# Row ends of a four-layer modulated convolution, as corrections subtracted at the end

## The chip, the cores and the metric

One core of one Trainium2 chip. The metric is the time of the program on the device in microseconds, the median of its runs. The engines are TensorE (PE, with its weight loads as PEld), VectorE (DVE), ScalarE (ACT), GpSimd (POOL), and SyncE (SP), which here issues nearly all DMAs.

## The reference

x is 128 x 64 x 1024 (batch, channels, length), fp32; cond_512 (128 x 128) is the style.

```python
def _layer(x, style, w, b, mw, mb, typ):
    s = style @ mw.T + mb
    weight = SCALE * w * s[:, None, :, None]
    demod = lax.rsqrt(jnp.sum(weight * weight, axis=(2, 3)) + EPS)
    weight = weight * demod[:, :, None, None]
    if typ == 'same':
        out = conv_same(x, weight) + b
    elif typ == 'upsample':
        out = conv_transpose(x, weight, stride 2) + b
        out = _blur(out, 2.0 * blur_k, (1, 1))
    elif typ == 'downsample':
        xb = _blur(x, blur_k, (2, 2))
        out = conv(xb, weight, stride 2) + b
    return out
...
for i, typ in enumerate(('same', 'upsample', 'same', 'downsample')):
    out = _layer(out, style, weights[i], biases[i], mod_w[i], mod_b[i], typ)
return x + out
```

Each batch element has its own 64 x 64 x 3 weights in every layer. Away from the row ends the four layers are one linear map: a convolution of seven taps of 64 x 64 matrices for each batch element, plus a constant. Within three columns of either end the zero padding of each layer makes the result differ from that convolution.

## The kernel before

**Tiling.** The batch is worked in 32 quads of four (NQ = 32, index q). A quad's two pairs lie side by side in a tile; in a pair, one batch element has partitions 0 to 63 (T) and the other 64 to 127 (Bo). All matmuls are fp32, 64 x 64, in the four quadrants of the array: row half r by column half c. HB is 64, half of the batch.

**The convolution.** x comes in three planes, columns of the same remainder modulo 3 (PL = 344 columns each, two pairs in X, double buffered). A short-convolution scheme makes five products a quad (conv0 to conv4, each 3 groups of four matmuls of NB = 340 columns) from sums of planes: in_g01 and in_g2 write G; in04, in1, in2 and in3 write the T tiles. VectorE does these, but in1 and in2, which run on GpSimd in the middle turns. The products are put together by copy_m3, sum1, sum2 and `output` (ScalarE, PSUM to the tile o, scaled and with the constant), and `store` sends o away. Ahead of this a chain of small matmuls (stage1, stage2, stage3, with combine_a and combine_b) makes the quad's seven-tap weights.

**Order.** The schedule is written out by hand. `turn_of(q)` holds, for q from 4 to 28, a whole turn: conv2, conv4 and conv0 of quad q, conv3 and conv1 of n = q+1, the weights of c = q+2 and s = q+4. `early_turn` does quads 0 to 3, and straight code the last three. Each engine runs its own instructions in program order. PSUM: two buffers for the products (psA; `banks(q)` is quad q's two banks), two banks Y, the rest for the weight chain. Tables SIDE, TABLES and SLOTS hang small work onto certain turns.

**The row ends.** They are computed apart. Eight columns of each end of x (Xe, with zero columns around them) are scaled by the style (setup_x) and go through the four layers for all 128 batch elements at once: ends0 in the slot of turn 10 gives six columns of layer 1, ends1 in turns 14 and 15 nine columns of layer 2 (five and four), ends2 in turn 19 eight columns of layer 3, three steps of the blur on VectorE (blur_side) in turns 22 to 27, and ends3 in the turn of q = 28. Each slot's matmuls go into Y (ends3: into psE), and rest0 to rest3 copy them to SBUF with a scale; add0, rest1_bias, rest1_edges and add2 add the biases. rest3_bias adds the bias and x in the last quads, and two stores send the three outer columns of each end. The convolution covers 1020 columns, of which 1018 are used. In the code of a slot turn:

```python
outputs(q, 0)
if q in SLOTS:
    matmuls, width, rest = SLOTS[q]
    slot(matmuls, width, Y_banks)
    rest()
...
conv1(n, ...)
sum1(n)
in3(c)
```

Lines that the profile names: L803 the convolution's products, L880 output on ScalarE, L712 sums with a factor (G, H, y, Y), L761 in3, L776 in1, L781 in2, L790 in04, L506 and L589 stage2, L428 stage1, L621 stage3, L1044 the end matmuls, L1146 and L1158 the last steps of the ends, L146 loads, L885 stores.

Of the kernel before, what the change touches and what calls it, by code (L numbers as in the profile page):

```python
# [63 lines left out]
def kernel(  # L64
# [74 lines left out]
    Xs = [const.tile([P, 2, NXC], F32, name=f"X{i}") for i in range(NX)]  # L139
# [24 lines left out]
    Xe = const.tile([P, B, 8], F32, name="Xe")  # L164
# [9 lines left out]
    NB = 340  # L174
# [578 lines left out]
    def g_tile(q):  # L753
        if q not in Gs:
            Gs[q] = gpool.tile([P, 2, 3 * PL], F32, tag="G", name=f"G{q}")
        return Xs[q % NX], Gs[q]
# [26 lines left out]
    def in04(q, pairs=BOTH_PAIRS):  # L783
        if q < NQ:
            t, g = t_tile(q, "T04"), Gs[q]
            a, b = g[:, pairs, :NJ], g[:, pairs, 2 * PL : 2 * PL + NJ]
# [3 lines left out]
            nc_v.tensor_sub(t[:, pairs, :, :NJ], both(a, PL), both(b, 1))  # L790
# [102 lines left out]
    WIDE = 6  # L893
    ends_ps = {}

    def slot(matmuls, n, ps, wide=WIDE):
        matmuls(ps)
        ends_ps[0] = ps, max(n, wide)

    def last(i, n, j):  # L900
        ps, w = ends_ps[0]
        return ps[i][:, : n * w].rearrange("c (b j) -> c b j", b=n)[:, :, :j]


# [81 lines left out]
    Xm = const.tile([P, B, 8], F32, name="Xm")  # L986
    Xs0 = [Xm[:, :HB], Xm[:, HB:]]
    a0, c0, a2, c2 = (const.tile([P, HB], F32, name=n) for n in ("a0", "c0", "a2", "c2"))
    g1 = const.tile([P, 6, C], F32, name="g1")

    Ye = [const.tile([P, HB, 8], F32, name=f"Ye{s}") for s in range(2)]
    Ue = [const.tile([P, HB, 11], F32, name=f"Ue{s}") for s in range(2)]
    Ve = [const.tile([P, HB, 12], F32, name=f"Ve{s}") for s in range(2)]
    Oe = const.tile([P, B, 3], F32, name="Oe")

    def zeros():
        for t in Ye:
            nc_g.memset(t[:, :, 0:1], 0.0)
            nc_g.memset(t[:, :, 7:8], 0.0)
        for t in Ue:  # L1000
            nc_g.memset(t[:, :, 0:1], 0.0)
            nc_g.memset(t[:, :, 10:11], 0.0)
        for t in Ve:
            nc_g.memset(t[:, :, 0:2], 0.0)
            nc_g.memset(t[:, :, 10:12], 0.0)
        nc_g.memset(g1, 0.0)

    def spread(t, n):

        return t[:, :, None].to_broadcast([P, t.shape[1], n])  # L1010
# [7 lines left out]
    def setup_x(h):  # L1018
        bs = slice(h * HB, (h + 1) * HB)
        nc_v.tensor_tensor(Xm[:, bs], Xe[:, bs], spread(sc[:, 0, bs], 8), op=ALU.mult)  # L1020

    def setup0():

        for rows, bs in ((T, slice(0, HB)), (Bo, slice(HB, B))):
            nc_v.tensor_mul(a0[rows], dm[rows, 1, bs], dm[rows, 0, bs])
            nc_v.tensor_copy(c0[rows], c0f[rows, bs])
# [4 lines left out]
    def setup3():  # L1031
        for rows, bs in ((T, slice(0, HB)), (Bo, slice(HB, B))):
            nc_v.tensor_copy(a2[rows], Da[rows, bs])
            nc_v.tensor_copy(c2[rows], c2f[rows, bs])

    def ends_matmul(ps, n, taps, weight, moving, wide=WIDE):
        for i in reversed(range(taps)):
            first = i == taps - 1
            w = max(n, wide)
            m = w if first else n  # L1040
            for r, rows in enumerate(HALF):
                for c, cols in enumerate(HALF):
                    dst = ps[r][cols, : HB * w].rearrange("c (b j) -> c b j", j=w)
                    nc.tensor.matmul(  # L1044
                        dst[:, :, :m],
                        weight(i, r, c)[rows],
                        moving(i, r, c, m)[rows],
                        start=first,
                        stop=(i == 0),
                        skip_group_check=True,  # L1050
                    )

    def ends0(ps):

        ends_matmul(
            ps, 6, K, lambda i, r, c: wio[0][:, i, :], lambda i, r, c, m: Xs0[c][:, :, i : i + m]
        )

    def rest0():
        for s in range(2):  # L1060
            dst = Ye[s][:, :, 1:7]
            nc_v.tensor_tensor(dst, last(s, HB, 6), spread(a0, 6), op=ALU.mult)

    def add0(s):
        dst = Ye[s][:, :, 1:7]
        nc_v.tensor_tensor(dst, dst, spread(c0, 6), op=ALU.add)

    def ends1(part):

        n = 5 - part  # L1070


        def weight(i, r, c):
            return g1[:, 2 * i + (part if c == 0 else 1 - part), :]

        def moving(i, r, c, m):
            col = 2 - i + (c + part if c else 0)
            return Ye[c][:, :, col : col + m]

        return lambda ps: ends_matmul(ps, n, K, weight, moving)  # L1080

    def rest1(part):
        n = 5 - part
        for h in range(2):
            bs = slice(h * HB, (h + 1) * HB)
            dst = Ue[h][:, :, 1 + part : 10 : 2]
            nc_v.tensor_tensor(dst, last(h, HB, n), spread(a1[:, bs], n), op=ALU.mult)

    def rest1_bias(h):

        bs = slice(h * HB, (h + 1) * HB)
        dst = Ue[h][:, :, 1:10]
        nc_v.scalar_tensor_tensor(
            dst, spread(b1s[:, bs], 9), 2.0, dst, op0=ALU.mult, op1=ALU.add
        )

    def rest1_edges(h):

        bs = slice(h * HB, (h + 1) * HB)
        for rows, col in ((T, 1), (Bo, 9)):  # L1100
            dst = Ue[h][rows, :, col]
            nc_v.scalar_tensor_tensor(
                dst, b1s[rows, bs], -0.25, dst, op0=ALU.mult, op1=ALU.add
            )

    def ends2(ps):

        ends_matmul(
            ps,
            8,  # L1110
            K,
            lambda i, r, c: wio[2][:, i, :],
            lambda i, r, c, m: Ue[c][:, :, i + r : i + r + m],
        )

    def rest2():
        for s in range(2):
            dst = Ve[s][:, :, 2:10]
            nc_v.tensor_tensor(dst, last(s, HB, 8), spread(a2, 8), op=ALU.mult)

    def add2(s):
        dst = Ve[s][:, :, 2:10]
        nc_v.tensor_tensor(dst, dst, spread(c2, 8), op=ALU.add)


    def blur_side(s, part):
        at = (2 * s, 0, 0)[part]
        src = (Ve[s], Ue[s], Ve[s])[part][:, :, at : at + 10 - part]
        dst = (Ue[s], Ve[s], Ue[s])[part][:, :, : 9 - part]
        nc_v.tensor_tensor(dst, src[:, :, :-1], src[:, :, 1:], op=ALU.add)  # L1130

    def ends3(ps):

        ends_matmul(
            ps,
            3,
            K,
            lambda i, r, c: wio[3][:, i, :],
            lambda i, r, c, m: Ue[c][:, :, i : i + 5 : 2],
            wide=3,  # L1140
        )

    def rest3():
        for h in range(2):
# [577 lines left out]
```

## Time and profile before

| | |
|---|---|
| median of 3 runs | 476.5 us (475.95 to 476.6) |
| span of the profiled execution | 475.5 us |
| PE busy | 469.7 us, 99% |
| VectorE busy | 417.3 us, 88% |
| ScalarE busy | 312.0 us, 66% |
| GpSimd busy | 165.8 us, 35% |
| granted TensorE clock, 40 slices | 0.9 or more in all |
| HBM | 145 GB/s over the span |

The page gives the span of the profiled execution, from its first to its last instruction; the time of that execution as a run isn't shown apart, so its span is set against the median of the runs, 1.0 us over it. Busy time counts an engine as busy while an instruction of it runs, and matmuls overlap. The chain that ended last is followed back from the last instruction; shares of the span by line come from it.

### The profile page before, as it was taken

How to read it: one execution, taken by the hardware profiler on the slowest of the kernel's cores; microseconds unless marked ns; L12 is line 12 of the kernel's file. 1: busy time of each engine (PE TensorE's matmuls, PEld its weight loads, DVE VectorE, ACT ScalarE, POOL GpSimd, SP SyncE). 2: the span in 40 equal slices, each digit the busy share in tenths (PEclk: the TensorE clock that was granted, in tenths of full speed). 3: DMA queues.
4: the chain of work that ended last, by engine and by line, in shares of the span. 5: the costliest groups of instructions: out<-in, count | busy, mean ns of one | idle time of the engine just before them, and what ended most of it. 6: DMA issues, size and time to landing. Idle time of an engine off the chain costs nothing.

```text
span 475.5 us, 26771 instructions
## 1 busy us (share of the span) xinstructions
PE 469.7 (99%) x11932; PEld 349.5 (74%) x11932; DVE 417.3 (88%) x694; ACT 312.0 (66%) x711; POOL 165.8 (35%) x200
## 2 busy tenths in 40 slices
PE   9999999999999999999999999999999999999996
PEld 6987788777678876677776677766788787876653
DVE  3889998879989998899979899979998999999896
ACT  4565657577766676766667666667666777766464
POOL 3634033664444342233432233422333423243200
PEclk9999999999999999999999999999999999999999
DMA  5237456535445554345544454543555544455225
GB/s 176 71 115 224 150 151 180 152 113 177 139 145 166 166 166 136 123 150 169 163 150 126 130 168 152 178 124 121 152 164 169 164 145 147 148 152 161 80 91 193
DMA packets 52707, 70.71 MB, mean 149 GB/s; under 512 B 6000, under 2 KB 50672, under 8 KB 52592
## 3 DMA queue, kind: packets, MB, share of 16 engines
q1 hardware_dynamic: 52368, 68.78, 46.3%
q8 instruction: 93, 1.52, 1.4%
q10 hardware_dynamic: 224, 0.22, 0.1%
q14 instruction: 22, 0.18, 0.1%
HBM read 35.36 MB, written 33.62 MB: 145 GB/s over the span
## 4 chain that ended last, share of the span: by engine, by line
PE 99%; DVE 0%; ACT 0%; issue 0%
PE psA L803 47%; PE Y L803 12%; PE psR L506 9%; PE psW L621 7%; PE psA L621 7%; PE psS L428 6%; PE psR L589 5%; PE psA L506 2%; PE Y L1044 2%; PE Y L183 1%; PE Y L379 1%; PE psM L220 0%; PE psE L1044 0%; PE Y L255 0%; DVE o L882 0%; PE psM L255 0%
## 5 line engine op out<-in xcount | busy, mean ns | idle before, releaser
L803 PE MATMUL psA<-T,H 64*64 64x340 f32 x2304 | 185.9, 446 | 0.0
L803 PEld LDWEIGHTS psA<-T,H 64*64 64x64 f32 x2304 | 90.7, 133 | 46.9 <-issue 2.5
L712 DVE SCALAR_TENSOR_TENSOR G<-X 128x1376 f32<-128x1376 f32 (+2 forms) x65 | 78.0, 1206 | 0.2
L776 POOL TENSOR_TENSOR T<-G 128x684 f32<-128x684 f32 x28 | 46.3, 1652 | 73.7 <-DVE G L712 73.7
L484 POOL TENSOR_TENSOR S<-S 128x128 f32<-128x128 f32 x28 | 21.6, 772 | 139.7 <-ACT S L399 139.6
L399 ACT ACTIVATE R<-psR,tC 128x448 f32<-128x448 f32 x63 | 36.6, 631 | 43.6 <-PE psR L506 25.8
L803 PE MATMUL psA<-T,Wf 64*64 64x340 f32 x768 | 63.7, 446 | 0.0
L803 PE MATMUL Y<-T,Wf 64*64 64x340 f32 x768 | 62.4, 451 | 0.0
L712 DVE SCALAR_TENSOR_TENSOR Y<-m,psA 128x340 f32<-128x340 f32 x62 | 32.0, 516 | 28.2 <-PE psA L803 26.9
L399 ACT ACTIVATE psW<-psA 128x128 f32<-128x128 f32 x100 | 19.3, 268 | 49.1 <-PE psA L621 45.0
L790 DVE TENSOR_TENSOR T<-G 128x1368 f32<-128x1368 f32 (+1 forms) x33 | 50.8, 1541 | 0.0
L399 ACT ACTIVATE Wf<-psW,t 128x256 f32<-128x256 f32 (+2 forms) x76 | 32.7, 480 | 26.7 <-PE psW L621 26.4
L761 DVE TENSOR_TENSOR T<-X 128x684 f32<-128x684 f32 x32 | 47.7, 1492 | 0.0
L506 PE MATMUL psR<-S,E 64*64 64x64 f32 (+1 forms) x1472 | 46.8, 237 | 0.0
L781 POOL TENSOR_TENSOR T<-G 128x684 f32<-128x684 f32 x28 | 46.5, 1660 | 0.0
L428 PEld LDWEIGHTS psS<-wd,w2n 64*64 64x64 f32 x1120 | 35.1, 133 | 12.9 <-issue 0.3
L506 PEld LDWEIGHTS psR<-S,E 64*64 64x64 f32 x1472 | 39.5, 134 | 4.9 <-ACT psR L529 0.2
L803 PEld LDWEIGHTS Y<-T,Wf 64*64 64x64 f32 x768 | 30.3, 132 | 16.8
L803 PEld LDWEIGHTS psA<-T,Wf 64*64 64x64 f32 x768 | 29.8, 133 | 14.5
L880 ACT ACTIVATE o<-psA,tb,td 128x340 f32<-128x340 f32 x63 | 37.1, 648 | 5.0 <-PE psA L803 2.8
L880 ACT ACTIVATE o<-y,tb,td 128x340 f32<-128x340 f32 x62 | 38.5, 678 | 0.0
L880 ACT ACTIVATE o<-Y,tb,td 128x340 f32<-128x340 f32 x62 | 36.1, 639 | 2.8 <-PE Y L803 2.0
(180 smaller groups left out, 840.4 us busy)
## 6 DMA issues: line engine op xcount, KB each, us to landing
out<-o SPq DMA_DIRECT2D x191, 170.0 KB, 2.6
X<-in_x SPq DMA_DIRECT2D x150, 172.0 KB, 3.4
X<-in_x SPq DMA_DIRECT2D x14, 516.0 KB, 5.0
par<-in_params SPq DMA_DIRECT2D x3, 192.0 KB, 3.8
Xe<-in_x_ends SPq DMA_DIRECT2D x1, 512.0 KB, 4.5
out<-Oe SPq DMA_DIRECT2D x2, 96.0 KB, 2.1
out<-o ACTq DMA_DIRECT2D x1, 170.0 KB, 2.8
par<-in_params SPq DMA_DIRECT2D x1, 160.0 KB, 2.7
```

The lines of the kernel that those rows point to most:

```text
L399: nc_a.activation(dst, src, AF.Copy, scale=f)
L428: nc.tensor.matmul(ps[r][cols, at * C : (at + n) * C], weight[rows], wd[c if r == 0 else 1 - c][rows, taps], start=first, stop=last, skip_ ...
L506: nc.tensor.matmul(dst[r][cols], weight[rows], st[c if r == 0 else 1 - c][rows, slots, :], start=False, stop=last, skip_group_check=True,)
L589: nc.tensor.matmul(ps[r][cols, lo * C : (lo + m) * C], E[rows, e + 2, :], src[rows, a, :], start=(n == 0), stop=(n == 8), skip_group_check ...
L621: nc.tensor.matmul(dst[r][cols], weight[rows], t[rows, c, slots, :], start=first, stop=last, skip_group_check=True,)
L712: nc_v.scalar_tensor_tensor(out, x, f, y, op0=ALU.mult, op1=op)
L761: nc_v.tensor_sub(t[:, pairs, 0, :NJ], plane(X, 3, pairs), plane(X, 1, pairs))
L776: eng.tensor_add(t[:, :, 0, :NJ], plane(g, 2), plane(g, 1))
L781: eng.tensor_sub(t[:, :, 1, :NJ], plane(g, 2), plane(g, 1))
L790: nc_v.tensor_sub(t[:, pairs, :, :NJ], both(a, PL), both(b, 1))
L803: nc.tensor.matmul(ps[s][cols, :NB], w, Ts[q, tag][rows, c, i, g : g + NB], start=(g == 0 and (m == 3 or alone)), stop=(g == K - 1), skip_ ...
L880: nc_a.activation(dst, src, AF.Identity, bias=add, scale=d3)
```

## The change

The convolution now covers 342 columns a plane (NB = 342), 1026 in all, over the zero-padded x: at the ends it gives the result that the seven taps alone would give. What it has too much there, because the layers' own padding cuts it off, is computed as a correction: three columns at each end of x (Xe, three columns in place of eight) go through the four layers in tiles that hold both ends mirrored, and the result Oe is subtracted from the convolution's outer columns. GpSimd copies these columns out of the output tile o (`gather`, two small operations a turn, for the quad before) into Oc. For quads 0 to 26 one subtraction on VectorE (correct_all, turn 28) and a store follow; from quad 27 on `correct` subtracts directly, the last quad's on VectorE, and a second store ends the program. The slots are now four: ends0 in turn 10, ends1 in 14, ends2 in 18, ends3 in 26. Their matmuls stand behind conv1(n), write banks(q) instead of Y, and their reading on VectorE follows sum1. The plane length PL stays 344; windows of 344 or 689 columns now run past a pair's end into the next pair or into 8 columns of zeros (`window`). Vectors by half of the batch that VectorE made (setup0, setup3) are made by GpSimd in turns 8 to 10 (end_tables).

```diff
-    NB = 340
+    NB = 342
...
-        return buf[:, pairs, at : at + NJ]
+        return window(buf, pairs, at, NJ)
...
-            sum_of(g[:, pairs, PL:], X[:, pairs, : 2 * PL], 0.5, X[:, pairs, PL:], ALU.subtract)
+            n = 2 * PL + 1
+            sum_of(
+                window(g, pairs, PL, n),
+                window(X, pairs, 0, n),
+                0.5,
+                window(X, pairs, PL, n),
+                ALU.subtract,
+            )
...
+    def ends_matmul(ps, n, moving, plan):
+        for i, (weight, src, dst) in enumerate(plan):
             for r, rows in enumerate(HALF):
                 for c, cols in enumerate(HALF):
+                    out_ = ps[r][cols, : HB * n].rearrange("c (b j) -> c b j", j=n)
+                    d = dst(r) if callable(dst) else dst
                     nc.tensor.matmul(
+                        out_[:, :, d],
+                        weight(r, c)[rows],
+                        moving[rows, c, :, src],
+                        start=(i == 0),
+                        stop=(i == len(plan) - 1),
                         skip_group_check=True,
                     )
...
     def ends0(ps):
+                (w[2], slice(0, 3), slice(0, 3)),
+                (w[1], slice(0, 2), slice(1, 3)),
+                (w[0], slice(0, 1), slice(2, 3)),
...
+    def ends1(ps):
+                (g[0], slice(2, 4), slice(1, 6, 4)),
+                (g[2], slice(1, 3), slice(1, 6, 4)),
+                (g[1], slice(1, 3), slice(0, 3, 2)),
+                (g[4], slice(0, 2), slice(3, 6, 2)),
+                (g[3], slice(1, 2), slice(2, 3)),
+                (g[5], slice(0, 1), slice(4, 5)),
...
+    def ends2(ps):
+                (w[0], slice(0, 5), slice(0, 5)),
+                (w[1], slice(1, 5), slice(0, 4)),
+                (w[2], slice(2, 5, 2), slice(0, 3, 2)),
+                (w[2], slice(5, 6), slice(1, 2)),
...
+    def ends3(ps):
+                (w[0], slice(0, 3, 2), lambda r: slice(0, 2 + r, 1 + r)),
+                (w[0], slice(4, 5), lambda r: slice(2 - r, 3 - r)),
+                (w[1], slice(1, 4, 2), lambda r: slice(0, 2 + r, 1 + r)),
+                (w[2], slice(2, 5, 2), lambda r: slice(0, 2 + r, 1 + r)),
...
+    def edges(q, planes):
+        o = os[q].rearrange("c r i j -> c r j i")
+        at, step = ((0, NB - 1), (0, NB - 2))[planes.start > 0]
+        return o[:, :, at : step + 1 : step, planes], 2 * q
+
+    LATER_ENDS = NQ - 5
+
+    def correct(q, planes, eng=nc_g):
+        src, b = edges(q, planes)
+        at = slice(b, b + 2)
+        if q < LATER_ENDS:
+            eng.tensor_copy(Oc[:, at, :, planes], src)
+        else:
+            eng.tensor_sub(Oc[:, at, :, planes], src, Oe[:, at, :, planes])
+
+    def gather(q):
+        for planes in (slice(1, K), slice(0, 1)):
+            correct(q, planes)
+
+    def correct_all(n):
+        nc_v.tensor_sub(Oc[:, : 2 * n], Oc[:, : 2 * n], Oe[:, : 2 * n])
+        store_ends(0, n)
...
+    SLOTS = {10: (ends0, rest0), 14: (ends1, rest1), 18: (ends2, rest2), 26: (ends3, rest3)}
...
+        28: lambda: correct_all(LATER_ENDS),
...
         outputs(q, 0)
-        if q in SLOTS:
-            matmuls, width, rest = SLOTS[q]
-            slot(matmuls, width, Y_banks)
-            rest()
-        if s == NQ:
-            slot(ends3, 3, unit(ps_w, "psE"), 3)
-            rest3()
         conv1(n, *((2,) if entry else range(K)))
         if q in SMALL:
             small(q)
+        if q in SLOTS:
+            SLOTS[q][0](banks(q))
         sum1(n)
+        if q in SLOTS:
+            SLOTS[q][1](A[q])
         in3(c)
-        side(LATE, q)
+        gather(q - 1)
...
+    correct(q, slice(1, K), nc_v)
     conv0(q, *range(K))
     for i, (eng, queue) in enumerate(zip(BOTH, (nc_a, nc.sync))):
         output(q, 0, i, eng)
         store(q, i, slice(0, 1), queue)
+    correct(q, slice(0, 1), nc_v)
+    store_ends(LATER_ENDS, NQ)
```

More of the change, by code (lines that the diff above doesn't have):

```diff
@@ L138, with pairs_of, window @@
     PL = NXC // 3
-    Xs = [const.tile([P, 2, NXC], F32, name=f"X{i}") for i in range(NX)]
+    def pairs_of(t):
+        return t[:, : 2 * NXC].rearrange("c (p n) -> c p n", p=2)
+    def window(t, pairs, at, n):
+        p0, p1 = pairs.start, pairs.stop
+        v = t[:, p0:p1, :]
+        return bass.AP(
+            v.tensor, v.offset + at, [*(list(d) for d in v.ap[:-1]), [1, n]]
+        )
+    Xs = [const.tile([P, 2 * NXC + 8], F32, name=f"X{i}") for i in range(NX)]
+    for t in Xs:
+        nc_g.memset(t[:, 2 * NXC :], 0.0)
+    Xs = [pairs_of(t) for t in Xs]
     def load(q, planes=slice(0, 3), cs=range(2)):
@@ L785, in in04 @@
             t, g = t_tile(q, "T04"), Gs[q]
[L786 removed]
+            a, b = window(g, pairs, 0, NJ), window(g, pairs, 2 * PL, NJ)
             both = lambda v, step: bass.AP(
@@ L1064, in add0 @@
[L1064 to L1087, printed above, removed]
@@ L1106, in ends2 @@
-    def ends2(ps):
+        w = [mirrored(wio[0], i, 1) for i in range(K)]
         ends_matmul(
             ps,
-            8,
             K,
-            lambda i, r, c: wio[2][:, i, :],
-            lambda i, r, c, m: Ue[c][:, :, i + r : i + r + m],
-        )
[L1116 to L1123, printed above, removed]
@@ L1126, in blur_side @@
[L1126 to L1132, printed above, removed]
+            Xm,
+            (
+                (w[2], slice(0, 3), slice(0, 3)),
+                (w[1], slice(0, 2), slice(1, 3)),
+                (w[0], slice(0, 1), slice(2, 3)),
+            ),
+        )
@@ L1584 @@
     outputs(q, 0)
+    for i in range(2):
+        for planes in (slice(1, K), slice(0, 1)):
+            correct(q - i, planes)
     conv2(n)
```

242 lines of the change are left out of this document (117 added, 125 removed).

## The prediction

> **What bounds the kernel now.** I read the busy table first, then the chain that ended last, then turns cut out by window, then the groups by shape.
>
> ```profile
> span 475.5 us, 26771 instructions
> PE 469.7 (99%) x11932; PEld 349.5 (74%) x11932; DVE 417.3 (88%) x694; ACT 312.0 (66%) x711; POOL 165.8 (35%) x200
> PE 99%; DVE 0%; ACT 0%; issue 0%
> 176.81:192.58 15.77, 15.77 (x413) 10.71 (x412) 12.94 (x25) 9.86 (x23) 4.81 (x5) 1.00 0.55 162
> 192.58:206.42 13.84, 13.84 (x388) 9.79 (x389) 12.73 (x20) 9.79 (x23) 4.82 (x5) 1.00 0.43 139
> 206.42:220.26 13.84, 13.84 (x388) 9.79 (x389) 12.73 (x20) 9.79 (x23) 4.81 (x5) 1.00 0.46 141
> ```
>
> The last three rows are whole turns, from one conv4 to the next: length, then busy time of PE, PEld, DVE, ACT and POOL, the granted clock (1.00) and the DMA share. PE fills each turn. A plain turn takes 13.84 us; the one at 176.81 holds one slot of end work and takes 1.93 us more. So a column more or less on PE is worth its own time, and work on VectorE or GpSimd is worth nothing unless PE comes to wait for it. The profiled execution has a span of 475.5 us against a median of 476.5: 1.0 us lies around the span, and I add it at the end.
>
> **Columns of the convolution.** Rows of the chain that ended last (start, length):
>
> ```profile
> 183.94 1.94 PE Y L1044 x24
> 203.37 1.72 PE psA L803 x24
> 241.25 1.73 PE Y L1044 x24
> 256.81 1.63 PE Y L1044 x22
> 313.93 2.60 PE Y L1044 x24
> 440.53 1.40 PE psE L1044 x24
> ```
>
> One product (24 records) of 340 columns takes 1.72 us, 5.06 ns a column. The page counts 2304+768+768 = 3840 records, so 160 products; two more columns in each cost 160 x 2 x 5.06 ns = **+1.62 us**. In the turns this is not hidden, since PE has no idle time there. VectorE gets the same 0.6%, 0.08 us of its 12.73 in a turn; this is covered by its wait of 0.86 us (row at 175.54 below).
>
> **End slots removed.** The four slots in Y (ends0, two of ends1, ends2) took 1.94+1.73+1.63+2.60 = **-7.90 us**. The turn at 176.81 confirms the first: 15.77-13.84 = 1.93. The fifth slot (ends3, 1.40 us) lies in the turn of q=28, and I treat it there.
>
> **End slots added.** Columns per quadrant, from the plans in the diff, times 64 batches: ends0 (3+2+1) 384, ends1 (2+2+2+2+1+1) 640, ends2 (5+4+2+1) 768, ends3 (2+1+2+2) 448, in all 2240 against 5184 before. At 1.94 us / (3 x 384) = 1.69 ns a column that would be 3.8 us, the lower end. But old ends3 has three taps of 192 columns, half of ends0, and took 1.40, not 0.97: it reads every second element of its rows, at 1.40/576 = 2.43 ns a column. All at that price is 5.45 us. Of the new columns 896 are read in runs of most of a row (ends0's 3 and 2 of 3, ends2's 5 and 4 of 6); the other 1344 are singles, pairs in rows of 4 or every second element. 896 x 1.69 + 1344 x 2.43 = 4.8 us; two more steps (17 against 15) and the writes below make me take **+5.0 us**, nearest to the strided row. Upper end: the new matmuls also write PSUM in steps of two and four elements. No row of before does that (the old writes leave out at most every sixth or two of six columns, and 64x320 stays on the line of 64x384), so I bound it by the strided price twice over for the 1344: 1.5+6.5 = 8.0.
>
> The Trainium skill ("Advanced Engine Details and Errata", section Memory Cachelines) says that any non-contiguous access to PSUM slows matmuls significantly, with lines of two fp32, and that SBUF needs two hits on a 16-byte line. The SBUF half agrees with the 1.40 us of old ends3; no run here shows the PSUM half.
>
> **A new wait on PE.** The old slot wrote Y, which was free. The new one comes behind conv1(n) and writes banks(q), which ScalarE still reads for outputs(q,0). Timeline rows of two turns:
>
> ```profile
> 171.00 1.18 ACT L880 ACTIVATE o<-psA,tb,td 128x340 f32<-128x340 f32 x2
> 171.64 0.40 PE L506 MATMUL psR<-S,E 64*64 64x128 f32 x8
> 414.70 1.19 ACT L880 ACTIVATE o<-psA,tb,td 128x340 f32<-128x340 f32 x2
> 415.46 0.40 PE L506 MATMUL psR<-S,E 64*64 64x128 f32 x7
> 175.54 1.07 DVE L712 SCALAR_TENSOR_TENSOR Y<-m,psA 128x340 f32<-128x340 f32 x2 [0.86 <-PE psA L803]
> ```
>
> Where stage2 now starts (171.64, 415.46), the slot would start. The second of the two outputs ends at 172.18 and 415.89, 0.54 and 0.43 us later; the first ends about when the slot starts, so only the second bank waits, but every step of the slot needs both. Queued behind the waiting matmul is all of PE: stage2, conv2 and on. I take 0.48 for each of four slots, **+1.9 us**; bounds 0 (ScalarE early) and 0.6 each. VectorE's reading of the slot (one instruction in place of two) now follows sum1; its lateness is covered by a turn that PE itself makes longer.
>
> **GpSimd gathers, and other covered work.** Two copies of 8 and 4 elements a turn.
>
> ```profile
> L332 POOL TENSOR_SCALAR tb<-oc 64x8 f32<-64x8 f32 x4 | 1.3, 327 | 8.6 <-DVE oc L977 8.5
> L930 POOL TENSOR_TENSOR Da<-sc,dm 128x16 f32<-128x16 f32 x2 | 2.3, 1156 | 0.2
> 429.96 1.65 POOL L776 TENSOR_TENSOR T<-G 128x684 f32<-128x684 f32 x1 [2.67 <-DVE G L712]
> 60.46 1.96 POOL L781 TENSOR_TENSOR T<-G 128x684 f32<-128x684 f32 x1
> 62.51 1.17 ACT L880 ACTIVATE o<-Y,tb,td 128x340 f32<-128x340 f32 x2 [0.72 <-ACT R L399]
> 172.62 4.36 SPq L146 DMA_DIRECT2D X<-in_x  x6
> 172.83 1.85 DVE L761 TENSOR_TENSOR T<-X 128x684 f32<-128x684 f32 x1
> X<-in_x SPq DMA_DIRECT2D x150, 172.0 KB, 3.4
> 182.25 0.86 DVE L712 SCALAR_TENSOR_TENSOR G<-X 128x684 f32<-128x684 f32 x1
> ```
>
> The nearest rows give 0.65 to 2.3 us for two, and GpSimd idles 2.67 us just there, waiting for G: nothing, unless they pass 2.7 us a turn; then in1 and behind it in3 slip. The table copies of turns 8 to 10, four small operations each, lie in its other wait, for S; without that cover they would cost by the same rows 1.3 to 4.6 us once a turn, and only as far as S comes late to stage2. Once there is no cover: in turn 2 output(2,2) at 62.51 needs the o buffer that gather(0), queued behind the in2 that ends at 62.42, still reads: +0.1 us (0 to 0.4). Loads: in3's window now reaches one column into the second pair, so the second of six issues waits for in3, where the third did. The third to sixth of today's issues lie between in3's end (174.68) and 176.98, 0.58 each; with five behind in3 the last is issued at 177.0 and lands 3.4 later, at 180.4, and in_g2 reads it at 182.25: nothing. On SP the first store of the ends waits for correct_all in the turn of q=28, and the output stores queued behind it wait for ScalarE anyway: nothing, with 0.3 us for the queue if not. The end input is smaller and needed late.
>
> **The turn of q=28.** Here VectorE and GpSimd nearly set the pace:
>
> ```profile
> 440.59 1.58 DVE L712 SCALAR_TENSOR_TENSOR G<-X 128x1376 f32<-128x1376 f32 x1
> 442.09 0.62 DVE L1146 SCALAR_TENSOR_TENSOR Oe<-psE,dm 128x192 f32<-128x192 f32 x2
> 443.79 0.87 DVE L712 SCALAR_TENSOR_TENSOR y<-psA,m 128x680 f32<-128x680 f32 x1 [1.08 <-PE psA L803]
> 442.35 1.65 POOL L776 TENSOR_TENSOR T<-G 128x684 f32<-128x684 f32 x1 [7.19 <-DVE G L712]
> 443.95 1.64 POOL L781 TENSOR_TENSOR T<-G 128x684 f32<-128x684 f32 x1
> 444.57 1.75 DVE L761 TENSOR_TENSOR T<-X 128x684 f32<-128x684 f32 x1
> 446.24 1.57 DVE L790 TENSOR_TENSOR T<-G 128x1368 f32<-128x1368 f32 x1
> 447.94 1.07 DVE L712 SCALAR_TENSOR_TENSOR Y<-m,psA 128x340 f32<-128x340 f32 x2
> 449.39 1.72 PE Y L803 x24
> L776 DVE TENSOR_TENSOR T<-G 128x684 f32<-128x684 f32 x4 | 3.6, 902 | 0.1
> L501 DVE TENSOR_TENSOR S<-S 128x256 f32<-128x256 f32 x23 | 9.6, 418 | 0.0
> ```
>
> L761 takes 1.75 us here and ends 0.73 after GpSimd's 445.59, though a subtraction of its size takes 0.90 (L776 on VectorE): it stands still while GpSimd reads. So G's end (442.17) starts a row of in1, in2, in3, in04 that end at 447.81, and then sum2 opens conv4 at 449.39. Taking ends3 out frees 1.40 us of PE and removes the wait of 1.08 and rest3 from VectorE, but not this row. And correct_all (324 elements, between 418 ns for 256 and 902 for 684: 0.47 us) is put ahead of in_g01, so G and the row come 0.47 later. PE arrives 1.4 us early at conv4, and waits: the 1.40 isn't gained, and conv2 of the turn after, which follows the same VectorE chain, comes **+0.45 us** later (bounds: -1.4 if the chain yields, +0.8).
>
> **The end.** One small correction on VectorE and a small store now follow the last output:
>
> ```profile
> 471.66 0.39 ACTq L885 DMA_DIRECT2D out<-o  x1
> out<-o ACTq DMA_DIRECT2D x1, 170.0 KB, 2.8
> out<-Oe SPq DMA_DIRECT2D x2, 96.0 KB, 2.1
> ```
>
> The old last store lands at 474.46. The new one can be issued near 472.1 and lands 2.1 later, 474.2: **+0.1 us**, bounds 0 and 0.6.
>
> **Sum.** 1.62 - 7.90 + 5.0 + 1.9 + 0.1 + 0.45 + 0.1 = +1.27 us; 475.5 + 1.3 = 476.8 span, and with the 1.0 around it **477.8 us**, 0.27% over the median.
>
> **Rivals.**
> - *Not slower: the turn of q=28 yields.* If in3 and in04 get between GpSimd's reads, PE keeps the 1.40: -1.85, so 475.9. For it: VectorE waits 1.08 there today. Against: L761's length. It decides if in04 ends more than 1 us before 447.8 on the old clock. Chance 0.13.
> - *The new matmuls stream at the plain price*, 3.8 us: -1.2, so 476.6. For: the 64x320 shape shows no penalty for rows of which a part is read. Against: old ends3. 0.14.
> - *ScalarE is in time*: the slot waits for nothing: -1.9, so 475.9. For: in slot turns VectorE has no side work ahead of the share copy. Against: the 0.43 is from a turn in which ScalarE has no gaps from m to o. 0.08.
> - *Two of these three together*: 474.8 or less. 0.10.
> - *PSUM writes in steps are slow*: half way to the upper end, 6.5 us: +1.5, so 479.3. Nothing in the profile for or against. 0.10. The rule of the Trainium skill named above speaks for it.
> - *My forecast*, 477.0 to 478.9 on its own: 0.45.
>
> **How the numbers follow.** A measurement of this kernel tells about 0.2% (0.95 us) from no change. Faster, under 475.55: the pair of rivals (0.10) and a third of the two near 475.9 (0.07), 0.17. Slower, over 477.45: the forecast but for its lower edge (0.43) and the PSUM rival, 0.53. The rest, 0.30. The range 475.1 to 479.4 leaves out a tenth on either side.
>
> **What would show it.** Plain turns of 13.89 us; products of 1.73; turns 10, 14, 18 and 26 longer than these by 1.2 to 2.1, with a hole of about 0.45 in the slot's matmuls that ScalarE's o ends; columns of the slots above 1.7 ns; in the turn of q=28 PE idle ahead of conv4 by over a microsecond, L761 long; GpSimd's wait for G shorter by the copies and not gone. Wrong it would be if PE does not wait in the last turns, if the slots cost under 4 us or over 6.5, or if GpSimd's copies take over a microsecond each and hold VectorE.

## The result, and the profile after

The changed kernel takes 512.97 us, median of six runs (510.79 to 517.83), against 476.23 us for the kernel before: ratio 1.0787, 95% interval 1.0748 to 1.0826. It is slower, as forecast, but by 36.7 us where 1.3 were forecast, and far above the range of 475.1 to 479.4.

The page of the changed kernel: the span, the busy times, and the queues of data and of instructions.

```profile
span 509.7 us, 26883 instructions
PE 476.9 (94%) x11948; PEld 367.0 (72%) x11948; DVE 414.0 (81%) x676; ACT 311.6 (61%) x711; POOL 179.3 (35%) x266
q1 hardware_dynamic: 52496, 68.65, 49.7%
q8 instruction: 93, 1.52, 1.4%
```

PE was busy 99% of the span before and is 94% now; no other engine has gained on it. The list of waits says where PE stands (total, times, longest):

```profile
PEld psA L634 <- issue: 17.2, 17, 3.1
PE psA L634 <- issue: 14.8, 13, 2.9
PE psR L519 <- issue: 2.6, 3, 1.3
ACT psW L412 <- PE psA L634: 62.8, 23, 4.9
```

The same two waits on stage3 in the kernel before:

```profile
PEld psA L621 <- issue: 0.3, 1, 0.3
ACT psW L399 <- PE psA L621: 45.0, 23, 2.4
```

L634 is stage3 (L621 before), L519 is stage2. "issue" means that nothing the profile shows released it: no semaphore, no tile. ScalarE's wait for the same matmuls, on the last row of each, grows behind it. Next, three turns cut out by window, from conv4 to conv4 (columns as in the prediction: length, busy time of PE, PEld, DVE, ACT, POOL, granted clock, DMA share, GB/s):

```profile
259.31:273.21 13.90, 13.90 (x391) 9.80 (x389) 12.76 (x20) 9.80 (x23) 5.38 (x7) 1.00 0.38 105
379.67:396.68 17.01, 14.07 (x394) 11.49 (x388) 15.64 (x26) 9.80 (x23) 5.16 (x6) 1.00 0.61 137
396.68:414.08 17.40, 15.88 (x392) 12.10 (x385) 11.44 (x18) 9.80 (x23) 4.73 (x6) 0.90 0.47 107
```

These are plain turns, without a slot. The first is as forecast (13.89). The second has the same PE work and 2.94 us of PE idle; in the third the mean clock is down to 0.90 and the same work takes 15.88 us. The timeline of the second, in the middle of stage3_b:

```profile
389.38 4.49 SPq L159 DMA_DIRECT2D X<-in_x  x6
392.14 1.00 PE L634 MATMUL psA<-R,w0s 64*64 64x192 f32 x24
392.90 0.34 PE L634 MATMUL psA<-R,par 64*64 64x64 f32 x7
396.18 0.27 PE L634 MATMUL psA<-R,par 64*64 64x64 f32 x1 [2.94 <-issue]
```

PE stops after seven of the eight records of one step, which read the same column block of R with the same weights. No operand can have come late between the seventh and the eighth. The same turn by stages, with the DMA engines' busy share and rate in the last two columns:

```profile
388.00:390.00 2.00, 2.00 (x93) 1.84 (x89) 2.00 (x3) 1.82 (x4) 0.98 (x1) 1.00 0.69 237
390.00:393.00 3.00, 3.00 (x92) 2.46 (x86) 1.95 (x3) 1.16 (x2) 1.53 (x3) 1.00 0.78 105
393.00:395.00 2.00, 0.24 (x14) 0.10 (x4) 2.00 (x4) 0.00 (x0) 1.48 (x1) 1.00 1.04 44
395.50:397.50 2.00, 1.32 (x37) 1.12 (x41) 1.93 (x5) 0.50 (x4) 0.00 (x0) 0.96 0.98 345
```

In the kernel before, the end of stage3_b in the corresponding turn:

```profile
378.00:380.00 2.00, 2.00 (x64) 1.70 (x60) 1.97 (x5) 0.76 (x5) 1.63 (x2) 1.00 0.82 243
```

Read share and rate together. While PE stands still, the DMA engines are busy all the time (1.04) and move 44 GB/s; two microseconds later they are as busy and move 345. The packets were stuck, and PE went on soon after they moved again. What PE waited for is told by the counts between the ends of five such stalls:

```profile
349.41:364.41 15.00, 14.02 (x383) 12.55 (x383) 12.60 (x20) 9.80 (x23) 4.92 (x7) 1.00 0.50 135
364.41:379.22 14.81, 14.34 (x382) 12.53 (x382) 11.51 (x19) 9.80 (x23) 4.31 (x6) 1.00 0.53 148
379.22:396.18 16.96, 14.02 (x383) 11.44 (x383) 15.63 (x26) 9.80 (x23) 5.56 (x7) 1.00 0.60 135
396.18:413.40 17.22, 15.70 (x382) 12.05 (x382) 11.26 (x17) 9.80 (x23) 4.73 (x6) 0.90 0.46 111
```

382 or 383 matmuls and as many weight loads: PE's instruction stream stops every 764 to 766 instructions, beside a few semaphore instructions that are not counted. With these, the trace has exactly 768 = 3 x 256 instructions of PE from each of these stops to the next. The page has 93 instruction packets of together 1.52 MB, 16.3 KB each, for 2 x 11948 PE instructions, one packet for every 257. So three packets make about a turn, and PE stops where one block of 256 instructions gives way to the next. The Trainium skill ("Runtime: NRT & Kernel Launch", section Instruction fetch mechanics) says that an engine's instructions are refilled in blocks of 16 KiB, 256 instructions, by a DMA queue of its own while the engine works on the block before, and calls the cost mostly hidden. The sizes agree with this trace; hidden it is in the kernel before, and not here. The recorded packet is not what overlaps the stop: the last instruction packet ahead of the stop of 2.94 us runs from 389.92 to 391.60, PE issues its last matmul at 393.02, and it goes on at 396.18, 4.6 us behind the packet's end. If that packet brings the block that PE stands for, what holds the block back comes behind the packet's record, and no record shows it.

So in the trace the loss begins with DMA engines that are busy and don't move. The experiments look for why.

### The profile page after: what moved, and what is told of

Its sections match the earlier page's. It is cut to its first block, busy times and chain, and to the rows that moved or that the text cites. A ratio compares the mean times of both kernels' runs of the same rounds, so it can differ in the third digit from the quotient of the medians.

```text
span 509.7 us, 26883 instructions
## 1 busy us (share of the span) xinstructions
PE 476.9 (94%) x11948; PEld 367.0 (72%) x11948; DVE 414.0 (81%) x676; ACT 311.6 (61%) x711; POOL 179.3 (35%) x266
## 3 DMA queue, kind: packets, MB, share of 16 engines
q8 instruction: 93, 1.52, 1.4%
## 5 line engine op out<-in xcount | busy, mean ns | idle before, releaser
L823 PE MATMUL psA<-T,H 64*64 64x342 f32 x2304 | 188.9, 448 | 0.3 <-DVE y L725 0.2
L725 DVE SCALAR_TENSOR_TENSOR G<-X 128x1378 f32<-128x1378 f32 (+2 forms) x65 | 78.7, 1212 | 0.3
L796 POOL TENSOR_TENSOR T<-G 128x688 f32<-128x688 f32 x28 | 46.5, 1661 | 67.3 <-DVE G L725 67.3
L823 PE MATMUL Y<-T,Wf 64*64 64x342 f32 x768 | 64.4, 457 | 2.0 <-DVE Y L725 2.0
L823 PE MATMUL psA<-T,Wf 64*64 64x342 f32 x768 | 64.7, 448 | 0.0
L810 DVE TENSOR_TENSOR T<-G 128x1376 f32<-128x1376 f32 (+1 forms) x33 | 52.5, 1592 | 0.0
L519 PE MATMUL psR<-S,E 64*64 64x64 f32 (+1 forms) x1472 | 49.2, 238 | 1.3 <-issue 1.3
L801 POOL TENSOR_TENSOR T<-G 128x688 f32<-128x688 f32 x28 | 47.1, 1682 | 0.0
L774 DVE TENSOR_TENSOR T<-X 128x688 f32<-128x688 f32 x32 | 47.0, 1470 | 0.0
L634 PEld LDWEIGHTS psA<-R,w0s 64*64 64x64 f32 x1000 | 35.1, 133 | 16.4 <-issue 9.0
L634 PE MATMUL psA<-R,w0s 64*64 64x128 f32 (+2 forms) x1000 | 39.5, 263 | 7.6 <-issue 7.0
L519 PEld LDWEIGHTS psR<-S,E 64*64 64x64 f32 x1472 | 41.4, 134 | 5.6 <-issue 2.0
L823 PEld LDWEIGHTS psA<-T,Wf 64*64 64x64 f32 x768 | 32.8, 134 | 12.3 <-ACT m L1661 0.2
L900 ACT ACTIVATE o<-psA,tb,td 128x342 f32<-128x342 f32 x63 | 37.3, 652 | 5.0 <-PE psA L823 2.8
```

Source lines behind the costliest of these rows:

```text
L519: nc.tensor.matmul(dst[r][cols], weight[rows], st[c if r == 0 else 1 - c][rows, slots, :], start=False, stop=last, skip_group_check=True,)
L634: nc.tensor.matmul(dst[r][cols], weight[rows], t[rows, c, slots, :], start=first, stop=last, skip_group_check=True,)
L725: nc_v.scalar_tensor_tensor(out, x, f, y, op0=ALU.mult, op1=op)
L774: nc_v.tensor_sub(t[:, pairs, 0, :NJ], plane(X, 3, pairs), plane(X, 1, pairs))
L796: eng.tensor_add(t[:, :, 0, :NJ], plane(g, 2), plane(g, 1))
L801: eng.tensor_sub(t[:, :, 1, :NJ], plane(g, 2), plane(g, 1))
```

## The experiments

Names that begin with a_ are the changed kernel with one edit, b_ the kernel before with one. A turn stores six times, each time 128 rows (one plane, one half, 64 channels of two batch elements): one packet a row. "Row" is the distance in DRAM from one plane's row to the next, "channel" from one partition's output to the next; "input row" is the distance from one partition's input to the next. Ratios are against runs of the kernel before made beside each kernel.

| kernel | row, bytes | channel, bytes | stored, bytes | input row, bytes | us | ratio to before |
|---|---|---|---|---|---|---|
| before | 1360 | 8160 | 1360 | 4128 | 475.4 to 476.2 | 1 |
| b_ch8192 | 1360 | 8192 | 1360 | 4128 | 476.09 | 1.0010 (0.9999 to 1.0021) |
| b_ch8208 | 1360 | 8208 | 1360 | 4128 | 479.30 | 1.0074 (1.0055 to 1.0093) |
| b_dram342 | 1368 | 8208 | 1360 | 4128 | 484.41 | 1.0199 (1.0180 to 1.0218) |
| b_rows342 | 1368 | 8208 | 1368 | 4128 | 511.51 | 1.0739 (1.0709 to 1.0769) |
| b_dram352 | 1408 | 8448 | 1360 | 4128 | 475.66 | 0.9994 (0.9980 to 1.0007) |
| changed | 1368 | 8208 | 1368 | 4128 | 512.97 | 1.0787 (1.0748 to 1.0826) |
| a_ch8224 | 1368 | 8224 | 1368 | 4128 | 479.34 | 1.0079 (1.0063 to 1.0096) |
| a_ch8304 | 1368 | 8304 | 1368 | 4128 | 478.17 | 1.0049 (1.0034 to 1.0064) |
| a_dram346 | 1384 | 8304 | 1368 | 4128 | 477.77 | 1.0044 (1.0030 to 1.0058) |
| a_dram348 | 1392 | 8352 | 1368 | 4128 | 478.69 | 1.0057 (1.0036 to 1.0078) |
| a_dram352 | 1408 | 8448 | 1368 | 4128 | 477.45 | 1.0029 (1.0013 to 1.0046) |
| a_rows344 | 1376 | 8256 | 1376 | 4128 | 478.88 | 1.0063 (1.0041 to 1.0085) |
| a_x4224 | 1368 | 8208 | 1368 | 4224 | 667.03 | 1.4019 (1.3974 to 1.4064) |
| a_x4224_d352 | 1408 | 8448 | 1368 | 4224 | 477.24 | 1.0036 (1.0016 to 1.0056) |

**First: the rows, the loads, or GpSimd.** Three theories went into these runs. R: the longer rows of the output slow the DMA engines. L: the loads are queued behind in3 and bunched. G: GpSimd's copies hold something up.

a_pairs (512.57 us) keeps the pairs of X and G apart, so that the second load no longer waits for in3:

```diff
-    Xs = [const.tile([P, 2 * NXC + 8], F32, name=f"X{i}") for i in range(NX)]
+    Xs = [const.tile([P, 2, NXC + 8], F32, name=f"X{i}") for i in range(NX)]
```

> The changed kernel, with the two pairs of X and of G kept 8 columns apart, so that in3's and in_g01's windows end in a column of their own and no longer reach into the second pair: the first two of the six loads no longer wait for in3. Theory L: 477 to 485 us, and the stalls of stage3_b go. Theory R: 513 (505 to 516), stalls as before. Theory G: 513.

It changed nothing: theory L, the one that starts from the step which the prediction had priced at nothing, falls.

b_rows342 (511.51 us) is the kernel before with nothing but longer output rows, NO = 342, in two fixed tiles and in DRAM:

```diff
-            os[q] = opool.tile([P, 2, K, NB], F32, tag="o", name=f"o{q}")
+            os[q] = o_two[q % 2]
...
-            out[q, :, s, planes.start * NB : planes.stop * NB],
+            out[q, :, s, planes.start * NO : planes.stop * NO],
```

> The kernel before, with only its output rows made as long as in the changed kernel: 342 columns (1368 bytes) in SBUF and in DRAM, the last two zero. All arithmetic stays at 340 columns. Theory R (the longer, less aligned rows slow the DMA engines, and with them the blocks of PE instructions): 495 to 515 us, store packets that overlap loads grow from 60 to over 70 ns on average, and PE stalls of 1 to 3 us appear in stage3_b. Theory L (the loads are queued behind in3 and bunched): 476 us, no stall. Theory G (GpSimd's copies hold something up): 476 us.

Nearly the whole loss (35.4 of 36.7 us) is there without any of the change's arithmetic, its GpSimd work or its slots, so theory G falls too, and with the same waits (L625 is stage3 in this kernel):

```profile
span 509.1 us, 26743 instructions
q1 hardware_dynamic: 52368, 68.98, 52.5%
PE psA L625 <- issue: 15.2, 14, 2.6
```

Its trace also shows that the loads suffer, which the edit doesn't touch: their packets of 1376 bytes take 104.3 ns on average, against 76.8 in the kernel before; the stores' packets take 69.4 against 61.7.

a_dram352 (477.45 us) and a_rows344 (478.88 us) do the reverse. a_dram352 moves the rows apart in DRAM (its edit is shown); a_rows344 makes them 344 columns long in SBUF and in DRAM, by the edit of b_rows342 with NO = 344:

```diff
-            out[q, :, s, planes.start * NB : planes.stop * NB],
-            os[q][:, s, planes].rearrange("c i j -> c (i j)"),
+            out[q, :, s].rearrange("c (i j) -> c i j", i=K)[:, planes, :NB],
+            os[q][:, s, planes],
...
-    [B // 4, 2 * C, 2, 6 * NBL]
+    [B // 4, 2 * C, 2, 6 * NBL + 30]
```

> The changed kernel, with the rows of the output 352 columns apart in DRAM (1408 bytes, so that each starts on a multiple of 64 bytes); 342 columns are stored, and SBUF is as it was. Theory R, if it is the DRAM side: 477 to 485 us; if it is the SBUF side: 513. Theory L: 513. Theory G: 513.

> The changed kernel, with output rows of 344 columns in SBUF and DRAM (1376 bytes, a multiple of 32, as the load's rows), the last two zero, all 344 stored. Theory R: 477 to 485 us, the turns back at 13.9. Theory L: 513. Theory G: 513.

With rows 352 columns apart in DRAM, and SBUF, arithmetic and packets as in the changed kernel, 35.5 of the 36.7 us are gone. Its page and its DMA issues (median us from issue to landing in the last column):

```profile
span 475.0 us, 26883 instructions
PE 466.4 (98%) x11948; PEld 346.2 (73%) x11948; DVE 412.7 (87%) x676; ACT 311.6 (66%) x711; POOL 184.2 (39%) x266
q1 hardware_dynamic: 52496, 68.65, 45.4%
out<-o SPq DMA_DIRECT2D x191, 171.0 KB, 2.0
X<-in_x SPq DMA_DIRECT2D x150, 172.0 KB, 3.3
```

Against this kernel the changed one has 34.7 us more span: PE is idle 32.8 us in place of 8.6 (span less busy time) and busy 10.5 us more with the same instructions, of which the turn at clock 0.90 alone holds 2. The changed kernel's page gives no landing times for its stores. Those of the kernel before:

```profile
out<-o SPq DMA_DIRECT2D x191, 170.0 KB, 2.6
```

**Second: what about the rows.** Theory R was now made sharper: a row's start must be a multiple of 16 bytes or more.

> The changed kernel with rows 346 columns apart in DRAM (1384 bytes: the starts are multiples of 8 bytes, no more, as with 342), 342 stored. Theory R (a row's start must be a multiple of 16 bytes or more): 505 to 518 us, stalls in stage3_b as before. Rival P (it is the one distance of 8208 bytes from channel to channel, by where that lands in DRAM; here it is 8304): 477 us.

> The changed kernel with rows 348 columns apart in DRAM (1392 bytes: the starts are multiples of 16 bytes, and every second one not of 32, as with the 1360 bytes of the kernel before), 342 stored. Theory R with 16 bytes: 477 to 478 us, and stores that land 2.6 us after issue, as before the change. Theory R with 32 or 64 bytes: 485 to 515 us.

a_dram346 refutes it: its starts are multiples of 8 and no more, and it takes 477.77 us. Its rival P, the distance of 8208 from channel to channel, was then tried on the kernel before, where it should have been slow, with an edit of the output's shape (and of the store's index to match):

```diff
-    [B // 4, 2 * C, 2, 6 * NBL]
+    [B // 4, 2 * C, 6 * 2 * NBL + 12]
```

> The kernel before with one number changed: the distance in DRAM from one channel's output to the next, 8208 bytes as in the changed kernel in place of 8160 (12 unused columns behind each channel's 2040). Rows are 1360 bytes, their starts multiples of 16 bytes. Rival P (the distance from channel to channel is what counts: the 128 packets of a store then fall into few places of DRAM): 495 to 518 us with the stalls in stage3_b. Theory R (alignment of the rows' starts): 476 us.

> The kernel before with 8192 bytes from channel to channel (8 unused columns). Rival P, if it is nearness to 8192: slower still than with 8208, 510 to 540 us. Rival P, if it is something else about 8208: 476 us. Theory R: 476 us.

> The changed kernel with the output's rows as they are, 342 columns one behind the other (starts at multiples of 8 bytes), and 8304 bytes from channel to channel in place of 8208 (24 unused columns behind each channel). Rival P: 477 to 479 us. Theory R: 505 to 518 us.

a_ch8304 agrees with P. b_ch8208 does not: 495 to 518 us were expected and 479.30 came, a small loss (3.6 us) with stores that land 3.5 us after issue in place of 2.6. b_ch8192 says that nearness to 8192 is not enough (476.09). Both conditions together remain: the distance of 8208 and rows of 1368. Two more runs took the rows apart.

> The kernel before, 340 columns stored, with its rows 342 columns apart in DRAM (1368 bytes; 8208 from channel to channel). The starts are those of the changed kernel, but packets are 1360 bytes and 8 bytes lie between rows. If the starts cause the loss (multiples of 8, together with 8208): 495 to 515 us. If it takes rows that touch, or packets of 1368: 476 to 480 us.

> The changed kernel, 342-column rows one behind the other, with 8224 bytes from channel to channel in place of 8208 (4 unused columns behind each channel). If it takes exactly 8208, or channels that touch: 477 to 479 us. If the neighbourhood of 8192 is slow for rows of 1368: 490 to 515 us.

At 8208, packets of 1360 bytes cost 3.6 us more than before when their starts are 1360 apart, 9.1 when 1368, and 35.4 when the packets are 1368 as well (each against the runs of before beside it). Sixteen bytes more from channel to channel take nearly all of it away (a_ch8224).

**Third: is it the store by itself?** a_x4224 leaves the output as the changed kernel has it and pads the input's rows in DRAM; a_off and a_off32 move the output as a whole inside a larger tensor:

```diff
-            out[q, :, s, planes.start * NB : planes.stop * NB],
+            out[64 + q * P : 64 + q * P + P, s, planes.start * NB : planes.stop * NB],
```

> The changed kernel with its output as it is (8208 bytes from channel to channel), and 4224 bytes from row to row of the input in DRAM in place of 4128 (24 unused columns behind each row). If the loads are slowed because loads and stores meet in the same few places of DRAM: 477 to 490 us. If the stores alone are enough to hold the DMA engines: 508 to 518 us.

> The changed kernel with its output moved by 64 channels (525312 bytes) inside a larger output tensor: rows, lengths, starts and distances are the same, only the distance in DRAM between what is loaded and what is stored at one time is another. If that distance causes the loss: 477 to 495 us. If the store's own pattern does: 508 to 518 us.

> The changed kernel with the input's rows 4224 bytes apart, as in a_x4224 (667 us), and the output's rows 352 columns apart (8448 bytes from channel to channel). If the loads at 4224 are slow by themselves: over 600 us. If it takes loads and stores together, each at its distance: 476 to 480 us.

> As a_off, with the output moved by 32 channels (262656 bytes) in place of 64. If the distance between loads and stores matters in steps smaller than that: a time other than 497.7 and 513, anywhere from 477 to 560. If a_off's gain was only that of not standing at the tensor's start: 495 to 500 us again.

a_x4224 was expected to be at least no worse, and took 667.03 us; its data queue is busy 57.6% of the span for the same bytes, and PE now stands ahead of stage2 far longer (L520). Its mean granted clock is 0.91, so part of the time is slower matmuls: of 149.9 us more span than the changed kernel's, PE is idle 101.4 and busy 48.5.

```profile
q1 hardware_dynamic: 52496, 68.65, 57.6%
PE psR L520 <- issue: 55.9, 23, 6.9
```

Yet the same loads are harmless beside stores at 8448 (a_x4224_d352, 477.24 us). So the loads are not slow by themselves: it takes both, each at its distance. Stores at 8208 without loads beside them were not tried. a_off took 497.69 us (ratio 1.0468, 1.0439 to 1.0497) and a_off32 509.73 (1.0697, 1.0663 to 1.0731): the same store pattern, and the loss falls by 15 us or by 3 when the output is moved. That the loss depends on loads and stores together is thereby shown. That they meet in DRAM is the likeliest reading; the tensors' addresses are not on record, and a move changes the output's own place as well as its distance from the input. By what rule of the addresses it happens stays open.

b_dram352 asked whether the kernel before suffers from the same thing:

> The kernel before with its rows 352 columns apart in DRAM (starts at multiples of 64 bytes), 340 stored. If only stalls of PE pass into the time, there is nothing to gain: 475.5 to 476.3 us, though the stores land sooner (2.0 in place of 2.6 us). If the 16-byte starts of the kernel before cost it too: under 475 us.

It does not: its stores land 2.0 us after issue in place of 2.6, and the time is the same.

**Fourth: the slots.** In a_slots_y (474.72 us, 0.9976, 0.9964 to 0.9988) the slots are ahead of conv1 and in Y again, on rows of 352. It leaves out part of the sum: in some columns conv4 replaces what sum2 put into Y, where it should add to it.

```diff
         outputs(q, 0)
+        if q in SLOTS:
+            SLOTS[q][0](Y_banks)
+            SLOTS[q][1](Y)
         conv1(n, *((2,) if entry else range(K)))
```

> The changed kernel with rows 352 apart in DRAM, and with the four slots put back where the kernel before has them: ahead of conv1, written to Y and read from there. It takes away the wait of each slot for ScalarE's output of plane 0 (holes of 0.66, 0.72, 0.72 and 0.68 us in the aligned kernel). If these holes are what they seem: 2.8 us less than 477.45, so 474.2 to 475.2 us. If another wait takes their place (VectorE's reading of the slot late, Y not free in time): 476 to 478 us.

> The kernel with rows 352 apart and the slots in Y ahead of conv1 (a_slots_y, where the slots leave some columns of Y without the mark that conv4 adds to what is there, so that sum2's part is lost in four groups), with four small matmuls of zeros behind each slot that is narrower than Y's 342 columns, 24 to 32 records in all fewer than one product; these make the columns whole. 0.1 us each by a product's 0.21 ns a column and matmul, so 474.7 + 0.3 = 475.0 us (474.4 to 475.6), against 475.8 of the kernel before and 477.45 with the slots behind conv1.

a_slots_y0, with the zeros that make Y whole, takes 474.15 us against 475.35: ratio 0.9970 (0.9958 to 0.9982). It is the fastest kernel here that leaves nothing out, and beats the kernel before by 0.30%. The four slot turns of a_dram352, then of a_slots_y0:

```profile
175.96:191.06 15.10, 14.89 (x418) 11.82 (x410) 11.84 (x20) 9.80 (x23) 7.17 (x11) 1.00 0.53 164
232.75:249.65 16.90, 15.81 (x440) 11.76 (x433) 12.15 (x20) 9.80 (x23) 5.12 (x7) 1.00 0.52 165
291.35:307.29 15.94, 15.67 (x423) 10.81 (x416) 12.01 (x20) 9.80 (x23) 5.07 (x7) 1.00 0.48 151
404.66:420.31 15.65, 15.42 (x426) 11.74 (x418) 11.81 (x21) 9.80 (x23) 5.07 (x7) 1.00 0.53 160
```

```profile
175.32:190.22 14.90, 14.90 (x425) 13.62 (x418) 11.71 (x20) 9.79 (x23) 7.14 (x11) 1.00 0.51 159
231.91:247.19 15.28, 15.28 (x441) 11.41 (x433) 12.07 (x20) 9.78 (x23) 5.07 (x7) 1.00 0.49 155
288.88:304.44 15.56, 15.56 (x432) 11.00 (x425) 11.93 (x20) 9.78 (x23) 5.07 (x7) 1.00 0.53 161
401.73:417.14 15.41, 15.41 (x432) 11.33 (x425) 11.73 (x21) 9.78 (x23) 5.05 (x7) 1.00 0.45 142
```

Every idle moment of PE in these turns is gone (busy time equals length). Most of the gain is in turn 14. The timeline of a_dram352 shows there, beside the wait for ScalarE that was forecast, a second stop, in the middle of stage2 (L519):

```profile
242.07 1.60 PE L1058 MATMUL psA<-Ye,g 64*64 64x128 f32 x48 [0.28 <-ACT o L900]
242.47 4.41 SPq L159 DMA_DIRECT2D X<-in_x  x4
246.18 0.39 PE L519 MATMUL psR<-S,wsq 64*64 64x64 f32 x11 [0.82 <-issue]
```

My reading, by the mechanism above: 48 short matmuls of ends1 straight ahead of stage2's short ones use up a block of instructions so fast that the next is late even where the rows do no harm. The trace fits: the stop stands at the edge of a block, a whole number of 256 instructions from the stops of the changed kernel, and the last instruction packet ahead of it ends at 244.93, only 0.2 us before PE issues its last matmul and 1.25 us before it goes on. With conv1's long matmuls between the two, in a_slots_y0, the stop is gone; no run moved only the short matmuls.

## Why the prediction was wrong, and where it was right

**The step that failed** is one that is not in the sum: the stores. The prediction carried two more columns through PE, VectorE and the end slots, but not into DRAM, where they move every row of the output. The runs show 35.4 us for the rows alone (b_rows342), nearly all of the loss. Its sentence on the loads, that the last "lands 3.4 later, at 180.4, and in_g2 reads it at 182.25: nothing", took the landing of 3.4 us from a trace with other rows. The order of the loads, which that sentence was about, was rightly priced at nothing (a_pairs). No row of before shows a load that is slowed by a store, and how much the size hangs on a few bytes (3.6 us in b_ch8208, 35.4 in b_rows342) makes it unlikely that one could have told it. What the page of before did show is a queue of 93 instruction packets, one for every 257 instructions of PE; that PE could come to wait for it was not asked. That the kernel is slower, as forecast, is luck: the forecast had it from other terms.

**The sum itself** can be read off a_dram352, which is the change without the harm: 1.36 us over the kernel before in the same series (477.45 against 476.09; 0.6 to 2.2 by the interval), where the sum says 1.27. That it comes so close is partly luck, because several terms erred and offset each other in part. The 1.0 us around the span, which the prediction took from two different executions, is about 1.8 where a run lists both; it stands on both sides of the difference.

- Columns: right. Plain turns of a_dram352 take 13.90 us (forecast 13.89). One of a_dram352, then of a_slots_y0:

```profile
218.85:232.75 13.90, 13.90 (x392) 9.77 (x384) 12.92 (x21) 9.88 (x23) 5.21 (x7) 1.00 0.47 152
```

```profile
218.02:231.91 13.89, 13.89 (x392) 9.76 (x384) 12.90 (x21) 9.86 (x23) 5.19 (x7) 1.00 0.50 160
```

- New slots: nearly right. In a_slots_y0 the four turns are longer than a plain one of 13.89 by 1.01, 1.39, 1.67 and 1.52, in all 5.59 with the zeros behind three of them (an unmeasured part of it); the forecast was 5.0. The 8.0 of PSUM writes in steps did not come, and with it the rule of the Trainium skill that the prediction weighed ("Advanced Engine Details and Errata", section Memory Cachelines): no run here shows that slowing for the PSUM side.
- The wait for ScalarE: there, in all four slots. 0.48 each was forecast, 1.9 in all, and PE is idle for 0.2 to 0.3 by the four rows of L1058 of a_dram352, 1.0 us in all (row below). But idle time understates it, since PE counts as busy until the matmuls already in it end. Without the wait the four turns are 2.44 us shorter (a_slots_y0), 1.6 of them beside the stop of 0.82 in turn 14, and that with the zeros in three turns:

```profile
PE psA L1058 <- ACT o L900: 1.0, 4, 0.3
```

- Turn 14 was to be longer by at most 2.1 and is by 3.0: the stop for instructions (0.82) had no term. With it, slots and waits make the four turns 8.0 us longer, where 5.0 and 1.9 were forecast.
- The turn of q = 28: its mechanism is right and its extra 0.45 is not. PE waits over a microsecond for the chain of VectorE and GpSimd, in04 (L810) is drawn out to 3.04 us, and the turn takes 14.76 us, as before (14.82). Rows of a_dram352:

```profile
434.21:448.97 14.76, 13.65 (x281) 9.24 (x273) 14.53 (x18) 8.53 (x19) 5.35 (x5) 1.00 0.38 126
444.20 2.28 POOL L801 TENSOR_TENSOR T<-G 128x688 f32<-128x688 f32 x1
444.89 3.04 DVE L810 TENSOR_TENSOR T<-G 128x1376 f32<-128x1376 f32 x1
448.97 1.38 PE L823 MATMUL Y<-T,Wf 64*64 64x342 f32 x16 [1.11 <-DVE Y L725]
```

- GpSimd's copies: 0.50 us a turn (forecast 0.65 to 2.3), hidden as said; correct_all 0.49 (forecast 0.47):

```profile
L1182 POOL COPY Oc<-o 128x8 f32<-128x8 f32 x27 | 8.1, 300 | 0.0
L1182 POOL COPY Oc<-o 128x4 f32<-128x4 f32 x27 | 5.3, 198 | 0.0
L1191 DVE TENSOR_TENSOR Oc<-Oc,Oe 128x324 f32<-128x324 f32 x1 | 0.5, 489 | 0.0
```

**Shown and argued.** That the output's rows in DRAM, by their length and distance, make 35 of the 37 us is shown by edits in both directions; that the input's distance bears on it is shown by a_x4224 beside a_x4224_d352. That the time passes through late blocks of PE instructions rests on the traces alone (the stop inside a run of equal matmuls, the spacing of 768, the DMA share beside the rate); no run changed the instruction stream without the rest. Of the 24.2 us of extra PE idle, 16.8 are waits for "issue" (17.9 us in the changed kernel, 1.1 in a_dram352), and 6.0 lie behind the last matmul, where the last outputs are made and the program waits for their stores: 10.1 us in the changed kernel, 4.1 in a_dram352. There, too, the lateness goes on behind the packets: in the changed kernel none moves after 504.8, and the span ends at 509.7; in a_dram352 it is 473.8 and 475.0. The last 1.4 us were not taken apart.

## What to carry to other kernels

When a change alters the length of a row that is stored, price the transfer as well as the arithmetic: look at the distances in DRAM of what is stored and of what is loaded beside it, and try another distance (a few unused columns) before judging the change. A PE that waits for "issue" in the midst of equal matmuls, at a fixed count of instructions, is most likely waiting for its instructions; look then at the DMA share beside the GB/s. And try runs of very short matmuls away from each other, with long ones between: here that went with the end of one stop of 0.82 us.

## What the runs showed of the hardware that was not expected

- Eight bytes of row length, 1360 to 1368, and with them 8160 to 8208 from channel to channel, cost 7.4% (b_rows342), and 96 bytes in the input's row distance, which are harmless beside stores at 8448, took the changed kernel from 513 to 667 us.
- The Trainium skill ("DMA: Bandwidth & Descriptors", section Latency and other measured facts) reports a rate that falls for transfers whose row distance in HBM is a large power of two, from 207 GB/s at 512 KiB to 103, half of the full rate, at 4 and 8 MiB, cured there by 4 KiB more and not by 192 bytes, and supposes that streams in step meet in the same channels. Here the distances are 4 to 8 KB, exactly 8192 is harmless with rows of 1360 bytes (476.09 us), 8208 costs 3.6 us with these and 35.4 with rows of 1368, 16 to 96 bytes more take nearly all of that away, and the loads matter as well as the stores. The supposed cause would fit; no run here shows it.
- In the turn that follows the stop of 2.94 us the mean granted clock is 0.90 (0.50 from 398.2 to 400.2), and the same matmuls keep PE busy 2 us longer; behind the stops of under 2 us shown here it stays at 1.00. A long stop can cost more than its length, but need not: in b_rows342 the clock is 0.50 behind a stop of 2.60 us (411.6 to 414.0) and 1.00 behind one of 2.51 (429.6 to 432.0).
